# Spacing the row gathers of a mixture-of-experts layer along TensorE's work

## The chip, the cores and the metric

One core of a Trainium2 chip runs the whole program in one launch. The metric is the device time in microseconds (us); a kernel is judged by the median of its timed runs. All arithmetic is in 32-bit floating point.

## The reference

The input is 32 images of 128 channels of 56 x 56 pixels. Two layers follow each other.

```
# layer 0 (mixture of experts)
x  = depthwise 7x7 convolution, layer norm over channels      # 100352 tokens of 128 values
each token takes its best 2 of 8 experts; tokens are served in order of priority,
an expert takes at most cap = 15680 tokens
y  = gelu(x @ W1 + b1) @ W2 + b2                              # 128 -> 512 -> 128
out = input + x + layer_scale * (gate1 * y[slot1] + gate2 * y[slot2])

# layer 1, on that output
feat = gelu(batchnorm(3x3 dilated convolution, 128 -> 64 channels))
F2   = fft2(feat); attention of 8 heads from its Gram matrix; a gate from its real part
out  = concat(|ifft2(attention * F2)|, |ifft2(gate * F2)|) + input
```

## The kernel before

Layer 0 first convolves and routes all tokens and leaves the normalised tokens in HBM as `xf`. Then the eight experts run one after the other. An expert takes its tokens in 31 chunks of 512: `expert` multiplies a chunk by `W1` in four products (`ph`, L1034), applies the GELU on ScalarE (`hT`, L1037), multiplies by `W2` in sixteen products (`py`, L1049), adds the bias on VectorE (`yo`, L1065), scales by the gates on ScalarE and writes the rows to `yf` in HBM through SP's queue. `tick` is called after every second group of products and fills in other work. Experts 0 to 6 read their tokens with indirect gathers issued by POOL (`xg`, L1010); the last expert's tokens were packed ahead and come with ordinary transfers (`xlast`).

To combine, every token needs the rows of `yf` at its two slots. The tokens are cut into 112 rows of 7 x 128 tokens (`NRB`). A row needs 14 gathers (`NG`), each of 128 tokens (`y`, L437), 1568 in all, issued by POOL. `release` asks for the next gather. At a row's first gather it also loads the row's own tokens (`xa`, L430) through SP. `total` puts a row's two additions on VectorE (`xa`, L453) and then the write to `xsum` (L454) through SP. `bring` loads a finished row back (`xs`, L476), and asks for whatever that row still lacks.

Gathers are not let loose. `marks` remembers, for each gather asked, the TensorE instruction that was the last one noted in `step["pe"]` at that time. Gather n then waits for mark n minus `leash["n"]`:

```
        marks.append(step["pe"])
        gated(marks[max(0, n - leash["n"])], nc.gpsimd.indirect_dma_start(
```

The leash is 4 while the last expert runs and 16 in layer 1. The gathers begin in the last expert, where `ahead` may ask for two at each of the first three ticks of a chunk and one at every other chunk's fourth, as far as the rows of `yf` they may touch (`reach`) are written two chunks before. Six `y` buffers hold seven gathers each, so three rows are in flight.

Layer 1 handles images in 16 pairs. `front` of a pair places the rows: `place` transposes them (`pxs`, L1236), VectorE adds them to the padded input `xp` (L1240), and `taps` convolves (`pf`, L1251), with the GELU on ScalarE (`feat`, L1259). `back` does the transforms, each as `turn` (transposes `pt`, L1294, copied by VectorE to `mid`, L1281) and `product` (`pm`, L1302), with the Gram matrix (`pg`, L1326), and the attention (`pre`, `pim`, L1391 and L1392). The generator `front` of the next pair is run between the steps of `back` of this one. Each generator yields an amount of work w at the end of a step, and `worked(w)` counts it; for every `PACE` of it one gather is asked, so that one step may ask several at the same mark.

`PACE` divides the counted work of a pair by 98 (2 NP) and multiplies by 1.07, so that a pair asks for fewer gathers than it uses; the head start from the last expert makes up for it until it is used up, and then `bring` asks for what is missing.

POOL, VectorE, ScalarE and SP each take their instructions in the order of issue. SP's queue in layer 1 carries the xa loads, xsum writes, xs loads, the padded inputs and the output, one behind the other. A gather that waits on POOL holds the ones behind it; a sum that waits on VectorE holds the copies behind it.

Of the kernel before, what the change touches and what calls it, by code (L numbers as in the profile page):

```python
# [45 lines left out]
E = 8  # L46
# [28 lines left out]
def conv_seq_kernel(ctx: ExitStack, tc: tile.TileContext, t: dict, out: bass.AP, dbg: dict):  # L75
# [320 lines left out]

    NRB = NI // 2 * NB
    NG = 2 * NB
    begun_ = {}
    marks = []  # L400
    leash = {"n": 4}
# [5 lines left out]
    def reach(r):  # L407

        return (E - 1) * cap + min(cap, (r + 1) * FW)
# [48 lines left out]
        while made_["summed"] < NRB and made_["asked"] >= (made_["summed"] + 1) * NG + lag:  # L458
            total()

    def worked(w):

        work["since"] += w
        while work["since"] >= PACE:
            work["since"] -= PACE
            release()
            totals(NB)

    def bring(r):
        if r >= NRB or r < made_["rows"]:  # L470
# [10 lines left out]
            nc.sync.dma_start(out=xps[i], in_=t["xp"][pr + i * HI])  # L481
        return xps

    def ahead(i, of):

        if of == 1:
            totals(NG)
        for k in range(2 if of < 4 else i % 2):
            if i * 512 < reach(made_["asked"] // NG) - (E - 1) * cap + 2 * 512:
                return  # L490
            release()

    slot1 = route2.tile([128, J], I32, name="slot1")
# [15 lines left out]
    if True:  # L509
# [514 lines left out]
                [(ns % 128, slice(full, full + 1))] if ns % 128 else []  # L1024
            )

        def expert(e, c0, gates, ns, xT, tick, before):


            hT = c2.tile([C, FF // C, 512], F32, name="hT")  # L1030
            mine = []
            for f in range(FF // C):
                ph = bank("ph")
                step["pe"] = nc.tensor.matmul(  # L1034
                    ph[:, :ns], lhsT=W1[:, e, f * C : (f + 1) * C], rhs=xT[:, :ns], start=True, stop=True
                )
                gelu = nc.scalar.activation(  # L1037
                    hT[:, f, :ns], ph[:, :ns], AF.Gelu, bias=b1t[:, e, f : f + 1]
                )
                mine.append(step["pe"])  # L1040
                if f % 2:
                    tick()
            with tc.issue_after(gelu.ins):
                before()
            py = bank("py")
            for q in range(-(-ns // 128)):
                n = min(128, ns - q * 128)
                for f in range(FF // C):
                    step["pe"] = nc.tensor.matmul(  # L1049
                        py[:n, q * C : (q + 1) * C],  # L1050
                        lhsT=hT[:, f, q * 128 : q * 128 + n],
                        rhs=W2[:, e, f, :],
                        start=(f == 0),
                        stop=(f == FF // C - 1),
                    )
                mine.append(step["pe"])
                if q % 2:
                    tick()
            mine += mine[-1:] * (8 - len(mine))
            spots.append(mine)  # L1060
# [24 lines left out]
            return after  # L1085
# [35 lines left out]
        for e in range(E):  # L1121
# [31 lines left out]

            def tick():
                state[0] += 1
                if e == E - 1:
                    state[2] += 1
                    ahead(i, state[2])
                with tc.issue_after(begun.ins):
                    while state[1] < len(todo) and state[2] * slots_ < state[0] * whole:  # L1160
                        todo[state[1]]()
                        state[2] += share.get(todo[state[1]], 0.7)
                        state[1] += 1

            for i, c0 in enumerate(chunks):
                if i + 1 < len(chunks):
                    then = fetch(ids, chunks[i + 1], e == E - 1)
                elif e + 1 < E:
                    then = fetch(ids2, 0, e + 1 == E - 1)
                if e in (E - 3, E - 2):  # L1170
                    for n in range(2):
                        if 2 * (i + (e - E + 3) * len(chunks)) + n < NC:
                            put(0, 2 * (i + (e - E + 3) * len(chunks)) + n)
                state[2] = 0 if e == E - 1 else state[2]
                left = expert(e, c0, gates, *now, tick, left)
                now = then
            assert state[1] == len(todo)
            if e + 1 < E:
# [50 lines left out]
    def place(r, xps):  # L1229
        xs, rb = rows.pop(r), r % NB  # L1230
        for m0 in range(0, NB, 4):
            nm = min(4, NB - m0)
            pt = bank("pxs")
            pv = pt[:, : nm * 128].rearrange("p (q m s) -> p q m s", m=nm, s=P8)
            for m in range(nm):
                nc.tensor.transpose(pv[:, :, m, :], xs[:, m0 + m, :], ident)  # L1236
            for i in range(2):
                px = interior(xps[i], rb * P8, P8)[:, :, m0 * P8 : (m0 + nm) * P8]
                pi = pv[:, i * P8 : (i + 1) * P8].rearrange("p r m s -> p r (m s)")
                step["dve"] = nc.vector.scalar_tensor_tensor(  # L1240
                    out=px, in0=pi, scalar=bC, in1=px, op0=ALU.add, op1=ALU.add
                )

    def front(pr, xps, feat):


        def taps(pf, g, k0):
            for k in range(k0, k0 + 3):
                o = ((k // 3) * 3 + 8 * g) * RP + (k % 3) * 3
                for i in range(2):  # L1250
                    step["pe"] = nc.tensor.matmul(  # L1251
                        pf[i * DD : (i + 1) * DD, : 8 * W],
                        lhsT=cw[:, k, :],
                        rhs=xps[i][:, o : o + 8 * RP].rearrange("p (h w) -> p h w", w=RP)[:, :, :W],
                        start=(k == 0),
                        stop=(k == 8),
                    )
            if k0 == 6:
                nc.scalar.activation(  # L1259
                    feat[:, 8 * g * W : 8 * (g + 1) * W], pf[:, : 8 * W], AF.Gelu, scale=bsc, bias=bsh  # L1260
                )
# [24 lines left out]
    def transform(src, n, m, by, to, copy, more=None):  # L1286
# [3 lines left out]
        def turn(i0):  # L1290
            ni = min(4, n - i0)
            pt = bank("pt")
            for i in range(ni):
                step["pe"] = nc.tensor.transpose(pt[:m, i * 128 : (i + 1) * 128], src(i0 + i), ident)  # L1294
            mid = ring.tile([128, 4, 128], F32, name="mid")
            dve(mid[:m, :ni, :].rearrange("p i c -> p (i c)"), pt[:m, : ni * 128])
            return i0, ni, mid

        def product(i0, ni, mid):
            pm = bank("pm")  # L1300
            for i in range(ni):
                step["pe"] = nc.tensor.matmul(  # L1302
                    pm[:, i * M : (i + 1) * M], lhsT=mid[:m, i, :], rhs=by, start=True, stop=True
                )
            copy(to(i0, ni), pm[:, : ni * M])  # L1305
            if more:
                more(i0, ni, mid)
# [11 lines left out]
    def back(pr, xps, feat):  # L1319
# [3 lines left out]

        def gram(j0, nj, F0):
            for j in range(nj):
                nc.tensor.matmul(  # L1326
                    pg, lhsT=F0[: 2 * W, j, :], rhs=F0[: 2 * W, j, :],
                    start=(j0 + j == 0), stop=(j0 + j == NT - 1),
                )

        yield from transform(
            lambda j: feat[:, j * 2 * W : (j + 1) * 2 * W], NT, 2 * W, rw,
# [53 lines left out]
        def attend(g):  # L1386
# [1 line left out]
            pre = bank("pre")  # L1388
            pim = bank("pim")
            ftf = feat[:, 8 * g * W : 8 * (g + 1) * W]  # L1390
            nc.tensor.matmul(pre[:, : 8 * W], lhsT=attn, rhs=ftf, start=True, stop=True)  # L1391
            step["pe"] = nc.tensor.matmul(pim[:, : 8 * W], lhsT=meanw, rhs=ftf, start=True, stop=True)  # L1392
            sr = d2.tile([128, 8 * W], F32, name="sr")
            nc.scalar.activation(sr, pre[:, : 8 * W], AF.Square)
            nc.scalar.activation(pim[:, : 8 * W], pim[:, : 8 * W], AF.Square)
# [90 lines left out]
    MAIN = 2 * (NT * (64 + 4 * KF) + KF * (64 + 4 * KF)) + NT * 128 + NB * 16 * W + 2 * -(-KF // 4) * 2 * KF  # L1486
    FRONT = NB * (NB * 64 + 9 * 8 * W)
    LEAD = MAIN // 6
    leash["n"] = 16
    PACE = (MAIN + FRONT) / (2 * NP) * 1.07  # L1490

    def pair(pr):
        return inputs(pr) if pr else first_inputs, d2.tile([128, NPIX], F32, name="feat")

    this = pair(0)
    for w in front(0, *this):
        worked(w)
    for pr in range(NI // 2):
        then, steps = None, iter(())
        if pr + 1 < NI // 2:  # L1500
# [3 lines left out]
        for w in back(pr, *this):  # L1504
            made += max(w, 0)
            goal = max(0, made - LEAD) * FRONT // (MAIN - LEAD)
            if w < 0:
                goal = max(goal, fed - w * 3 * 8 * W)
            worked(max(w, 0))
            while fed < goal:  # L1510
                f = next(steps, None)
                if f is None:
                    break
                fed += f
                worked(f)
        for w in steps:
            worked(w)
        this = then


# [122 lines left out]
```

## Time and profile before

| what | value |
|---|---|
| timed runs, median of 3 | 4856.02 us (4854.89 to 4864.45) |
| profiled execution | 5281.71 us |
| its span, first to last instruction | 5279.9 us |
| mean granted TensorE clock | 0.948 |
| first gather of `yf`, last expert | 2733 us |
| first transpose of layer 1 | 2989 us |
| gathers of `yf`: number, mean recorded time | 1568, 992 ns |
| two additions of a row: each | 1086 ns |

A page of the profile gives busy time per engine, then the costliest groups of instructions: line, engine, operation, tile written from tiles read, count, then busy time and mean duration, then the idle time of the engine just ahead of them and what ended most of it. Windows give the same sums for stretches of the span. In the chain of waits each step is followed back to what released it. The profiled execution is longer than the timed ones, so sums from it are made against its own time.

### The profile page before, as it was taken

How to read it: one execution, taken by the hardware profiler on the slowest of the kernel's cores; microseconds unless marked ns; L12 is line 12 of the kernel's file. 1: busy time of each engine (PE TensorE's matmuls, PEld its weight loads, DVE VectorE, ACT ScalarE, POOL GpSimd, SP SyncE). 2: the span in 40 equal slices, each digit the busy share in tenths (PEclk: the TensorE clock that was granted, in tenths of full speed). 3: DMA queues.
4: the chain of work that ended last, by engine and by line, in shares of the span. 5: the costliest groups of instructions: out<-in, count | busy, mean ns of one | idle time of the engine just before them, and what ended most of it. 6: DMA issues, size and time to landing. Idle time of an engine off the chain costs nothing.

```text
span 5279.9 us, 87289 instructions
## 1 busy us (share of the span) xinstructions
PE 4709.7 (89%) x32984; PEld 3221.7 (61%) x32984; DVE 2802.5 (53%) x5764; ACT 2111.7 (40%) x4260; POOL 2668.8 (51%) x2640
## 2 busy tenths in 40 slices
PE   7888835999999999999999899999998888888889
PEld 7777723777767777666666555555555554555556
DVE  4787787748585866431112235555554444444456
ACT  3576741444444444434443323333332222333234
POOL 0000043545554555666636666666666666666650
PEclk9999966999999999999999999999999899999999
DMA  9998940222222222233355546555555555565642
GB/s 254 272 264 253 268 109 22 64 66 64 65 64 64 67 65 67 76 92 87 89 167 154 136 123 161 159 159 161 159 161 156 157 159 147 138 162 153 166 137 58
DMA packets 767255, 705.22 MB, mean 134 GB/s; under 512 B 72752, under 2 KB 679089, under 8 KB 762741
## 3 DMA queue, kind: packets, MB, share of 16 engines
q1 hardware_dynamic: 596580, 487.54, 31.2%
q0 software_dynamic: 81664, 167.15, 14.0%
q10 hardware_dynamic: 88592, 44.96, 3.0%
q8 instruction: 261, 4.28, 0.3%
q14 instruction: 158, 1.29, 0.1%
HBM read 472.99 MB, written 226.39 MB: 132 GB/s over the span
## 4 chain that ended last, share of the span: by engine, by line
PE 59%; issue 10%; another core or an unknown queue 4%; POOL 4%; DVE 4%; ACT 3%; DMA 1%; DVEq 0%; POOLq 0%; SPq 0%; ACTq 0%
PE pf L1251 14%; PE py L1049 12%; PE ph L1034 11%; PE pm L1302 8%; PE pt L1294 4%; POOL xg L1010 3%; PE pg L1326 2%; ACT hT L1037 2%; PE pxs L1236 2%; PE pre L1391 2%; PE pim L1392 1%; PE pxt L1016 1%; DMA xg<-xf,ids 1%; DVE mid L1281 1%
## 5 line engine op out<-in xcount | busy, mean ns | idle before, releaser
L437 POOL DMA_INDIRECT y<-yf,slot x1568 | 1555.0, 992 | 902.0 <-issue 366.2
L1010 POOL DMA_INDIRECT xg<-xf,ids x861 | 939.0, 1091 | 781.9 <-PE ph L1034 436.1
L1037 ACT ACTIVATE hT<-ph,b1t 128x512 f32<-128x512 f32 (+1 forms) x992 | 655.5, 682 | 1241.4 <-PE ph L1034 1119.0
L1049 PEld LDWEIGHTS py<-W,hT 128*128 128x128 f32 x7872 | 958.2, 194 | 245.6 <-ACT hT L1037 149.1
L1049 PE MATMUL py<-W,hT 128*128 128x128 f32 x7872 | 1035.9, 283 | 59.0 <-ACT hT L1037 35.4
L1251 PE MATMUL pf<-xp,cw 128*64 128x448 f32 x4032 | 917.9, 562 | 6.5 <-issue 5.2
L1034 PE MATMUL ph<-xT,W 128*128 128x512 f32 (+1 forms) x1984 | 899.4, 593 | 2.9 <-issue 2.8
L1065 DVE TENSOR_TENSOR yo<-py,b2t 128x512 f32<-128x512 f32 (+2 forms) x256 | 170.2, 667 | 896.0 <-issue 739.2
L1281 DVE COPY mid<-pt 112x512 f32<-112x512 f32 (+3 forms) x480 | 311.1, 661 | 594.3 <-remote 213.7
L1034 PEld LDWEIGHTS ph<-xT,W 128*128 128x128 f32 x1984 | 357.5, 192 | 335.8 <-issue 331.4
L1251 PEld LDWEIGHTS pf<-xp,cw 128*64 128x64 f32 x4032 | 283.8, 138 | 436.6 <-issue 400.6
L217 POOL TENSOR_SCALAR y<-y,sd,nb 128x128 f32<-128x128 f32 x49 | 24.8, 519 | 689.6 <-DVE nb L209 689.6
L222 ACT ACTIVATE y<-y,nb,sd 128x128 f32<-128x128 f32 x735 | 288.7, 480 | 76.3 <-DVE nb L209 76.3
L1075 ACT ACTIVATE yo<-yo,gates 128x128 f32<-128x128 f32 (+1 forms) x984 | 312.4, 394 | 5.6 <-issue 3.8
L1305 ACT COPY T<-pm 128x464 f32<-128x464 f32 (+2 forms) x240 | 123.1, 520 | 458.4 <-PE pm L1302 316.2
L171 PE MATMUL psa<-xt,stay 112*64 112x98 f32 (+1 forms) x4608 | 235.6, 261 | 43.6 <-DVE y L179 23.8
L171 PEld LDWEIGHTS psa<-xt,stay 112*64 112x64 f32 (+1 forms) x4608 | 219.4, 145 | 60.5 <-DVE y L179 28.0
L1240 DVE SCALAR_TENSOR_TENSOR xp<-pxs,beta,xp 128x256 f32<-128x256 f32 x448 | 173.1, 445 | 135.2 <-PE pxs L1236 59.8
L453 DVE TENSOR_TENSOR xa<-xa,y 128x896 f32<-128x896 f32 x224 | 243.2, 1086 | 2.8
L1259 ACT ACTIVATE feat<-pf,bn_shift,bn_scale 128x448 f32<-128x448 f32 x112 | 81.0, 724 | 404.7 <-remote 195.7
L179 DVE TENSOR_TENSOR y<-psa,dwbB 128x392 f32<-128x392 f32 x256 | 140.8, 558 | 188.1 <-PE psa L171 150.9
L1302 PE MATMUL pm<-ih,mid 116*128 116x112 f32 x928 | 151.2, 311 | 96.2 <-DVE mid L1281 71.3
(410 smaller groups left out, 6211.1 us busy)
## 6 DMA issues: line engine op xcount, KB each, us to landing
xt<-in_x_dram SPq DMA_DIRECT2D x256, 392.0 KB
yf<-yo SPq DMA_DIRECT2D x240, 256.0 KB
xp<-in_xp_dram SPq DMA_DIRECT2D x32, 1832.0 KB
xa<-xf SPq DMA_DIRECT2D x112, 448.0 KB
xsum<-xa SPq DMA_DIRECT2D x112, 448.0 KB
xs<-xsum SPq DMA_DIRECT2D x112, 448.0 KB
xf<-y ACTq DMA_DIRECT2D x42, 1024.0 KB
y<-yf,slot POOLq DMA_INDIRECT x1568
```

What stands on the lines that cost most here:

```text
L171: nc.tensor.matmul(ps[h * 64 : (h + 1) * 64, c * TG : (c + 1) * TG], lhsT=wts[b][:, c4 + c, :], rhs=xv[: PKS[b], c, h, :, b * NB : b * NB ...
L222: nc.scalar.activation(yi, yi, AF.Identity, scale=sd[:, i : i + 1], bias=nb[:, i : i + 1])
L437: gated(marks[max(0, n - leash["n"])], nc.gpsimd.indirect_dma_start(out=begun_[r][1][-1][:, m, :], out_offset=None, in_=yf[: 1 + reach(r), :],
L453: nc.vector.tensor_tensor(out=xs, in0=xs, in1=y, op=ALU.add)
L1010: paced(q, nc.gpsimd.indirect_dma_start(out=xg[:n, q, :], out_offset=None, in_=xf, in_offset=bass.IndirectOffsetOnAxis(ap=ids[:n, c0 + q : ...
L1034: step["pe"] = nc.tensor.matmul(ph[:, :ns], lhsT=W1[:, e, f * C : (f + 1) * C], rhs=xT[:, :ns], start=True, stop=True)
L1037: gelu = nc.scalar.activation(hT[:, f, :ns], ph[:, :ns], AF.Gelu, bias=b1t[:, e, f : f + 1])
L1049: step["pe"] = nc.tensor.matmul(py[:n, q * C : (q + 1) * C], lhsT=hT[:, f, q * 128 : q * 128 + n], rhs=W2[:, e, f, :], start=(f == 0), sto ...
L1075: nc.scalar.activation(yo[:n, q], yo[:n, q], AF.Copy, scale=gates[:n, c0 + q : c0 + q + 1])
L1251: step["pe"] = nc.tensor.matmul(pf[i * DD : (i + 1) * DD, : 8 * W], lhsT=cw[:, k, :], rhs=xps[i][:, o : o + 8 * RP].rearrange("p (h w) -> ...
L1281: step["dve"] = nc.vector.tensor_copy(to, of)
L1302: step["pe"] = nc.tensor.matmul(pm[:, i * M : (i + 1) * M], lhsT=mid[:m, i, :], rhs=by, start=True, stop=True)
```

## The change

A gather is now asked for at the TensorE instruction that completes a pace of work. `beat(w, ins)` replaces `worked`: it notes the instruction as the mark, counts a weight for it (10 for a transpose, 19 for a transform or Gram product, 32 for a convolution product, 64 for an attention product), and asks for a gather when a pace is full. The transposes of `place` and the Gram products, which set no mark before, do now. The pace is the sum of these weights over a pair, divided by 98, times 1.1. The sums are asked for by `totals(NB)` at the ends of steps as before, but no longer within the loop of gathers. The leash in layer 1 is 8. In the last expert `ahead` is called after each of the four `ph` products and each of the four groups of `py`, and asks for one gather each time that `reach` allows; the sums of that expert are asked for ahead of each chunk.

```diff
-    def worked(w):
-
+    def beat(w, ins):
+
+        step["pe"] = ins
         work["since"] += w
         while work["since"] >= PACE:
             work["since"] -= PACE
             release()
-            totals(NB)
...
-    def ahead(i, of):
-
-        if of == 1:
-            totals(NG)
-        for k in range(2 if of < 4 else i % 2):
-            if i * 512 < reach(made_["asked"] // NG) - (E - 1) * cap + 2 * 512:
-                return
+    def ahead(i):
+
+        if i * 512 >= reach(made_["asked"] // NG) - (E - 1) * cap + 2 * 512:
             release()
...
                 mine.append(step["pe"])
+                spot()
                 if f % 2:
                     tick()
...
                 mine.append(step["pe"])
+                spot()
                 if q % 2:
                     tick()
...
-                left = expert(e, c0, gates, *now, tick, left)
+                if e == E - 1:
+                    totals(NG)
+                left = expert(e, c0, gates, *now, tick, left, lambda: ahead(i) if e == E - 1 else None)
...
-                nc.tensor.transpose(pv[:, :, m, :], xs[:, m0 + m, :], ident)
+                beat(TURN, nc.tensor.transpose(pv[:, :, m, :], xs[:, m0 + m, :], ident))
...
-    leash["n"] = 16
-    PACE = (MAIN + FRONT) / (2 * NP) * 1.07
+    leash["n"] = 8
+    PACE = (4 * (NT + KF) * (TURN + PROD) // 2 + NT * PROD + 2 * NB * WIDE + NP * TURN + 18 * NB * TAP) / (2 * NP) * 1.1
...
     for w in front(0, *this):
-        worked(w)
+        totals(NB)
```

The other products (`pf`, `pt`, `pm`, `pg`, `pre`, `pim`) are wrapped in `beat` in the same way, and the other calls of `worked` become `totals(NB)`.

More of the change, by code (lines that the diff above doesn't have):

```diff
@@ L398, in conv_seq_kernel @@
     NG = 2 * NB
+    TURN, PROD, TAP, WIDE = 10, 19, 32, 64
     begun_ = {}
@@ L1025, in spans, with expert @@
             )
-        def expert(e, c0, gates, ns, xT, tick, before):
+        def expert(e, c0, gates, ns, xT, tick, before, spot):
             hT = c2.tile([C, FF // C, 512], F32, name="hT")
@@ L1155, in tick @@
                 state[0] += 1
-                if e == E - 1:
-                    state[2] += 1
-                    ahead(i, state[2])
                 with tc.issue_after(begun.ins):
@@ L1173, in conv_seq_kernel @@
                             put(0, 2 * (i + (e - E + 3) * len(chunks)) + n)
-                state[2] = 0 if e == E - 1 else state[2]
-                left = expert(e, c0, gates, *now, tick, left)
+                if e == E - 1:
+                    totals(NG)
+                left = expert(e, c0, gates, *now, tick, left, lambda: ahead(i) if e == E - 1 else None)
                 now = then
@@ L1250, in taps @@
                 for i in range(2):
-                    step["pe"] = nc.tensor.matmul(
+                    beat(TAP, nc.tensor.matmul(
                         pf[i * DD : (i + 1) * DD, : 8 * W],
@@ L1256, in taps @@
                         stop=(k == 8),
-                    )
+                    ))
             if k0 == 6:
@@ L1293, in turn @@
             for i in range(ni):
-                step["pe"] = nc.tensor.transpose(pt[:m, i * 128 : (i + 1) * 128], src(i0 + i), ident)
+                beat(TURN, nc.tensor.transpose(pt[:m, i * 128 : (i + 1) * 128], src(i0 + i), ident))
             mid = ring.tile([128, 4, 128], F32, name="mid")
@@ L1301, in product @@
             for i in range(ni):
-                step["pe"] = nc.tensor.matmul(
+                beat(PROD, nc.tensor.matmul(
                     pm[:, i * M : (i + 1) * M], lhsT=mid[:m, i, :], rhs=by, start=True, stop=True
-                )
+                ))
             copy(to(i0, ni), pm[:, : ni * M])
@@ L1325, in gram @@
             for j in range(nj):
-                nc.tensor.matmul(
+                beat(PROD, nc.tensor.matmul(
                     pg, lhsT=F0[: 2 * W, j, :], rhs=F0[: 2 * W, j, :],
                     start=(j0 + j == 0), stop=(j0 + j == NT - 1),
-                )
+                ))
         yield from transform(
@@ L1390, in attend @@
             ftf = feat[:, 8 * g * W : 8 * (g + 1) * W]
-            nc.tensor.matmul(pre[:, : 8 * W], lhsT=attn, rhs=ftf, start=True, stop=True)
-            step["pe"] = nc.tensor.matmul(pim[:, : 8 * W], lhsT=meanw, rhs=ftf, start=True, stop=True)
+            beat(WIDE, nc.tensor.matmul(pre[:, : 8 * W], lhsT=attn, rhs=ftf, start=True, stop=True))
+            beat(WIDE, nc.tensor.matmul(pim[:, : 8 * W], lhsT=meanw, rhs=ftf, start=True, stop=True))
             sr = d2.tile([128, 8 * W], F32, name="sr")
@@ L1508, in conv_seq_kernel @@
                 goal = max(goal, fed - w * 3 * 8 * W)
-            worked(max(w, 0))
+            totals(NB)
             while fed < goal:
@@ L1514, in conv_seq_kernel @@
                 fed += f
-                worked(f)
+                totals(NB)
         for w in steps:
-            worked(w)
+            totals(NB)
         this = then
```

## The prediction

> **What bounds the kernel now.** I read the page first, then the windows by stage, the waits of POOL, the chain of the last expert, and one timeline.
>
> ```profile
> PE 4709.7 (89%) x32984; PEld 3221.7 (61%) x32984; DVE 2802.5 (53%) x5764; ACT 2111.7 (40%) x4260; POOL 2668.8 (51%) x2640
> ...
> L437 POOL DMA_INDIRECT y<-yf,slot x1568 | 1555.0, 992 | 902.0 <-issue 366.2
> ...
> L453 DVE TENSOR_TENSOR xa<-xa,y 128x896 f32<-128x896 f32 x224 | 243.2, 1086 | 2.8
> ```
>
> TensorE is the busiest engine. The sums that use the gathers never waited for them: 2.8 us of idle in 224. So a gather is not late anywhere; what it can do is disturb TensorE, or sit badly. The windows are four stretches of layer 1:
>
> ```profile
> 3200.00:3600.00 400.00, 369.65 (x2185) 223.81 (x2183) 201.14 (x348) 128.51 (x215) 254.91 (x253) 0.95 0.59 158
> 3600.00:4000.00 400.00, 369.15 (x2187) 222.07 (x2184) 203.60 (x349) 130.47 (x217) 260.35 (x259) 0.97 0.59 160
> 4000.00:4400.00 400.00, 346.88 (x2012) 214.22 (x2010) 187.15 (x321) 112.97 (x190) 254.77 (x258) 0.93 0.57 154
> 4400.00:4800.00 400.00, 351.87 (x2012) 213.41 (x2012) 192.47 (x325) 114.83 (x193) 255.77 (x263) 0.94 0.59 158
> ```
>
> The first bracket is TensorE's instructions, the fifth POOL's. From 4000 us on TensorE gets through 8% less work (2012 against 2186) while POOL does as many gathers per us. That is the main lead. In the order of the built program, between the first attention products (L1391) of one pair and the next, POOL's gathers wait for marks of that pair 86 times in each of the first six pairs and 96 to 98 times in each of the next eight. By the starts of L1391 in the timeline, the first six take 133.3, 135.3, 135.7, 140.9, 133.2 and 132.6 us (mean 135.2), the next eight 146.8 to 154.6 (mean 149.8). The pace of 1.07 falls behind; from the seventh pair each row's remaining gathers are forced by `bring`, several on one mark.
>
> ```profile
> POOL y L437 <- issue: 324.0, 1033, 2.9
> POOL y L437 <- PE pm L1302: 146.6, 123, 3.6
> ```
>
> In layer 1, 1033 gathers followed the one before after 0.3 us of issue: POOL works in back-to-back runs of 1.25 us a gather. The longest stalls are of this kind, at 4109, 4264, 4416 and 5010 us, all in the later pairs:
>
> ```profile
> 4118.19 0.72 ACT L1259 ACTIVATE feat<-pf,bn_shift,bn_scale 128x448 f32<-128x448 f32 x1 [17.35 <-remote]
> ...
> 4120.38 0.98 PE L1302 MATMUL pm<-ih,mid 116*128 116x112 f32 x3 [10.96 <-DVE mid L1281]
> ```
>
> The convolution that this GELU waits for is recorded as ended at 4107.96; a gather that waits for the same product started at 4118.43, after a run of 17 back-to-back gathers. The last expert shows the same with nothing else changed:
>
> ```profile
> 2715.21 3.44 PE ph L1034 x8
> ...
> 2722.92 3.44 PE ph L1034 x8
> ...
> 2730.63 3.44 PE ph L1034 x8
> ...
> 2738.34 4.75 PE ph L1034 x8
> ...
> 2758.03 8.23 another core or an unknown queue x2
> ```
>
> A chunk takes 7.71 us until the first y gathers (2733 us); then 10 to 15 us alternates with 7.7.
>
> **What the Trainium skill says.** "Perfetto Trace Analysis", section "DMA Instruction — SWDGE (GPSIMD)": a gather's recorded time ends with its descriptors, not its data. The trace agrees: 0.99 us recorded, while the bytes of its queue, counted in order, land 5.4 us (median) and at most 10.8 us after its start. "TensorE: Matmul & The Clock Gate", table at its head: the queue is 64 deep, so a record may stand ahead of the work; the gather held until 4118 by a product recorded as over at 4107.96 agrees. Same page, "The cost: per-tile semaphore tail": about 26.3 ns per increment. The trace doesn't show that: after a convolution product that raises the semaphore the next starts 0.376 us later, after one that doesn't 0.376 (medians).
>
> **The change part by part.** The matmuls and their order stay but for 276 of 18813 places; what moves is which product each gather waits for, where sums stand, and thus the SP and DVE order.
>
> 1. Last expert. 6.5 gathers a chunk become 8. Gathers whose mark is ahead of layer 1's first transpose: 191 before, 218 after, +27. Price: from 2750 to 2950 us TensorE did 921 instructions; a chunk has 44 (8 of L1034, 32 of L1049, 4 of L1016) and takes 7.71 us undisturbed, so 921 are 161 us of work and 39 us were lost beside 135 gathers, 0.29 us each: 27 x 0.29 = +8 us. Upper end: the slope of step 3, 1.24 us, +33.
> 2. Pairs 1 to 6: 86 gathers become 89 to 90, about +3.2 each, 19 in all. At 0.29 us +6, at 1.24 us +24. I take +8.
> 3. Pairs 7 to 12: 96 to 98 become 89 to 90; the 13th 93; the 14th stays at 98. Slope between the two groups: (149.8 - 135.2) / (97.8 - 86) = 1.24 us a gather. Six pairs x 8.5 x 1.24 = -63, the 13th 5 x 1.24 = -6: -69. Lower end, if only the 0.29 counts: -16. The forcing by `bring` is over except in the last two pairs, and 1250 of 1293 marks carry one gather where 452 of 859 did (from gather 220), so I stay near the full: -60.
> 4. Semaphore. Products that raise it go from 5189 to 6204. By the trace nothing; by the skill's price an estimate of 1015 x 26.3 ns = 27 us if all were on the path. I take 0, keeping 0 to 27.
> 5. POOL's extra waits: 445 more semaphore instructions at 0.02 us are 9 us spread over 2400 us on an engine that stood waiting for others some 440 us in layer 1. 0.
> 6. Leash 16 to 8. A gather may start later, so the sum is nearer. Static distance from the awaited product to the sum, on before's times: least 17.6 us before, 9.9 after; median 31.8 before, 23.9 after. Measured slack from landing to the second addition was 10.4 us at least; less 7.7 it is 2.7. Cost 0. If that cover went, the DVE sum would wait, behind it `mid` and `xp`, then TensorE; and SP, which holds the xsum write and what is queued behind it. At most ten rows x 3 us = 30. Waiting gathers also hold later gathers on POOL; the same slack covers them.
> 7. SP: xsum writes and xa loads move by a few places; TensorE wants their rows two rows later, some 18 us. At layer 1's start the small loads (beta, cw) stay behind the same two xs loads, so that 8.8 us stall stays: 0.
>
> Sum: +8 + 8 - 60 = -44 us on the profiled 5281.71 (span 5279.9 plus 1.8 around it). The timed runs are shorter: median 4856.02, 0.92 of it. Scaled: -40, so **4816 us**. The profile may exaggerate the disturbance, since what it adds (425 us) is of the size of 1568 x 0.28 us.
>
> **Rivals.** (a) Forecast: late bunching goes, -40; for it the 8% drop at 4000 us and the stalls there alone. (b) The cost is a fixed price per gather wherever it stands: 1.24 in all steps gives +33 + 24 - 69 = -12, scaled -11, 4845; for it, that gathers per us are the same in all four windows; against it, 0.29 in the last expert. (c) Disturbance is mostly the profile's own: nothing but the ends stays, 4856 +- 9. (d) Slower: POOL becomes the bound of the last expert. Eight gathers need 8 x 1.25 = 10.0 us a chunk. That decides once a chunk takes under 10 us and the backlog exceeds the 14 to 22 places between ask and sum (about 20 us). With unprofiled chunks at 8.2 us (the mean of experts 1 to 4 in the profile, by the starts of L1034) the backlog is 26 x 1.8 = 47 us, 27 over the slack, and DVE holds TensorE by that: +27, plus 0 to 15 of steps 4 and 6, with layer 1 gaining little: about 4888. Against it: 9.5 us a chunk in the profile. That the change doesn't do what it says is excluded by the order of the marks.
>
> **How the numbers follow.** (a) 0.55, (b) 0.15, (c) 0.12, (d) 0.18. About 0.2% (10 us) is what a measurement of this kernel can tell from no change. Faster: all of (a) and half of (b) and a bit of (c), 0.66; same: the rest of (b) and (c), 0.16; slower: 0.18. (a) alone spans 4770 to 4843: the lower end if pairs 7 to 13 become like 1 to 6 in full (7 x 14.6 = -102, with +8 scaled -86), the upper if half of step 3 comes (-30 + 16, scaled -13). The range takes in (b) and (c) and half of (d): 4765 to 4872.
>
> **What would show it.** Right: TensorE's instructions per 400 us alike (about 2150) up to 4900 us; pairs 7 to 12 near 138 us; TensorE's waits of 10 us and more for `mid` gone; fewer than 1033 back-to-back gathers; last expert's chunk 9.6 to 10 us. Wrong: pairs still at 150 us with 89 gathers (the bunching wasn't it); L453 with tens of us of idle (leash too short or rival d); chunk beyond 10.5 us; layer 1 as before in the profile and yet slower runs.

## The result, and the profile after

| kernel | median of the timed runs | ratio to before, 95% interval |
|---|---|---|
| before | 4860.24 us (14 runs, 4854.89 to 4865.42) | |
| changed | 4867.59 us (14 runs, 4863.34 to 4874.26) | 1.0015 [1.0008, 1.0022] |

The forecast was 4816 us. The changed kernel is some 7 us slower, within what was called the same. Three more comparisons are told below: two repeat this, and in the last one, on another chip, the change was 40 us faster than the kernel before, the difference that was forecast. The result lies inside the range of the prediction, 4765 to 4872 us, but by luck: the range reached so far up only to take in half of rival (d).

The profiled execution of the changed kernel took 4864.57 us, so it stands for the timed ones. That of before, 5281.71 us, didn't: it is 8.7% above the median of the timed ones. The kernel before was therefore profiled again (first experiment): 4862.44 us. The comparison of stages uses this second profile.

The page of the changed kernel, the lines that answer to those shown of before:

```profile
PE 4528.4 (93%) x32984; PEld 3139.9 (65%) x32984; DVE 2801.9 (58%) x5764; ACT 2140.0 (44%) x4260; POOL 2682.7 (55%) x2640
...
L438 POOL DMA_INDIRECT y<-yf,slot x1568 | 1566.7, 999 | 566.3 <-issue 231.1
...
L454 DVE TENSOR_TENSOR xa<-xa,y 128x896 f32<-128x896 f32 x224 | 243.7, 1088 | 138.6 <-DMA y<-yf,slot 126.4
```

The sums, which had not waited in the first profile (2.8 us), now wait 138.6 us, nearly all for a gather's data. The windows of the changed kernel say where TensorE (first bracket) is short:

```profile
2750.00:2950.00 200.00, 150.75 (x795) 100.20 (x794) 49.13 (x82) 61.58 (x123) 153.37 (x154) 0.87 0.60 150
3200.00:3600.00 400.00, 400.00 (x2545) 250.57 (x2543) 234.32 (x403) 142.24 (x236) 300.91 (x303) 1.00 0.70 191
3600.00:4000.00 400.00, 399.99 (x2444) 238.35 (x2444) 230.18 (x393) 152.62 (x251) 295.99 (x296) 1.00 0.67 180
4000.00:4400.00 400.00, 399.99 (x2467) 242.19 (x2466) 234.43 (x403) 146.50 (x244) 297.14 (x296) 1.00 0.66 177
4400.00:4800.00 400.00, 397.30 (x2451) 243.70 (x2450) 224.96 (x385) 138.91 (x231) 254.50 (x252) 0.99 0.59 160
```

In layer 1 TensorE is full. Around the end of the last expert, 2750 to 2950 us, it is busy for three quarters of the time (150.75 of 200 us).

### The profile page after: what moved, and what is told of

The parts are those of the page before. It is cut to its first block, busy times and chain, and to the rows that moved or that the text cites. A ratio compares the mean times of both kernels' runs of the same rounds, so it can differ in the third digit from the quotient of the medians.

```text
span 4862.8 us, 87748 instructions
## 1 busy us (share of the span) xinstructions
PE 4528.4 (93%) x32984; PEld 3139.9 (65%) x32984; DVE 2801.9 (58%) x5764; ACT 2140.0 (44%) x4260; POOL 2682.7 (55%) x2640
## 5 line engine op out<-in xcount | busy, mean ns | idle before, releaser
L1034 ACT ACTIVATE hT<-ph,b1t 128x512 f32<-128x512 f32 (+1 forms) x992 | 676.1, 682 | 1100.3 <-PE ph L1031 1074.0
L1047 PEld LDWEIGHTS py<-W,hT 128*128 128x128 f32 x7872 | 940.6, 192 | 169.3 <-issue 121.3
L1047 PE MATMUL py<-W,hT 128*128 128x128 f32 x7872 | 987.1, 279 | 21.4 <-DVE yo L1064 21.1
L1248 PE MATMUL pf<-xp,cw 128*64 128x448 f32 x4032 | 880.8, 548 | 8.2 <-DVE xp L1237 7.8
L1064 DVE TENSOR_TENSOR yo<-py,b2t 128x512 f32<-128x512 f32 (+2 forms) x256 | 170.1, 667 | 714.2 <-issue 642.4
L454 DVE TENSOR_TENSOR xa<-xa,y 128x896 f32<-128x896 f32 x224 | 243.7, 1088 | 138.6 <-DMA y<-yf,slot 126.4
L1013 PE MATMUL pxt<-ident,xg 128*128 128x128 f32 (+1 forms) x984 | 195.2, 278 | 27.5 <-DMA xg<-xf,ids 27.5
```

Of the source, the lines that this page charges most:

```text
L454: nc.vector.tensor_tensor(out=xs, in0=xs, in1=y, op=ALU.add)
L1034: gelu = nc.scalar.activation(hT[:, f, :ns], ph[:, :ns], AF.Gelu, bias=b1t[:, e, f : f + 1])
L1047: step["pe"] = nc.tensor.matmul(py[:n, q * C : (q + 1) * C], lhsT=hT[:, f, q * 128 : q * 128 + n], rhs=W2[:, e, f, :], start=(f == 0), sto ...
L1248: beat(TAP, nc.tensor.matmul(pf[i * DD : (i + 1) * DD, : 8 * W], lhsT=cw[:, k, :], rhs=xps[i][:, o : o + 8 * RP].rearrange("p (h w) -> p h ...
```

## The experiments

The expectations speak of Theory P and Theory M. P is rival (d) of the prediction: eight asks in a chunk are more than POOL can issue, the sums on VectorE wait, and TensorE behind them. M: the semaphore raises of the moved marks cost time, at the price estimated in step 4 of the prediction. Every other letter is explained in the expectation that uses it; Theory S of the first experiment is not the rival S of the later ones. Ratios are to the kernel before on the same chip.

**The kernel before, once more.**

> The kernel before, unchanged, profiled once more. Theory S (the stalls of the first profile belonged to that execution, and layer 1 is full of TensorE work): a span near 4860 us, TensorE busy over 398 of 400 us between 3200 and 4400, pairs at 119 to 122 us whether 86 or 98 gathers fall in them. Theory F (the prediction: forced, bunched gathers slow TensorE): again above 5200 us, or, if shorter, pairs 7 to 14 at least 5 us longer than pairs 1 to 6.

Measured: 4862.44 us. Its windows and the line of its sums:

```profile
2750.00:2950.00 200.00, 189.47 (x1116) 123.69 (x1115) 61.57 (x109) 71.72 (x142) 152.73 (x156) 0.97 0.63 161
3200.00:3600.00 400.00, 399.99 (x2441) 238.85 (x2441) 228.21 (x392) 153.49 (x253) 290.11 (x293) 1.00 0.65 176
3600.00:4000.00 400.00, 399.60 (x2460) 241.19 (x2456) 238.11 (x408) 144.54 (x240) 299.80 (x299) 1.00 0.68 183
4000.00:4400.00 400.00, 385.47 (x2332) 231.60 (x2332) 223.80 (x379) 135.11 (x225) 306.02 (x307) 0.99 0.66 181
4400.00:4800.00 400.00, 384.39 (x2382) 237.13 (x2379) 213.93 (x366) 135.46 (x226) 256.96 (x255) 0.99 0.58 155
```

```profile
L453 DVE TENSOR_TENSOR xa<-xa,y 128x896 f32<-128x896 f32 x224 | 243.8, 1088 | 109.2 <-DMA y<-yf,slot 98.6
```

In the stretches from 3200 and from 4000 us the first profile had 2185 and 2012 instructions of TensorE, and this one has 2441 and 2332. TensorE is full up to 4000 us, and the sums wait already before the change. The chunks of the last expert take 7.7 us to the end (the first 8.4). By the starts of the attention products (L1391), the pairs take 119 to 122 us up to the ninth (the first 124.5), then 130.0, 127.3, 126.6, 129.9 and 126.9: the late pairs are longer by some 7 to 8 us here, not 15. So neither theory holds whole: the span is that of Theory S, but pairs 10 to 14 are longer than the early ones by more than the 5 us of Theory F.

**Each part alone.** Only the last expert's part:

```diff
-                    ahead(i, state[2])
...
+                if e == E - 1:
+                    totals(NG)
+                left = expert(e, c0, gates, *now, tick, left, lambda: ahead(i) if e == E - 1 else None)
```

> Only the last expert's part of the change: eight asks a chunk, one at each product group. Theory P (POOL cannot keep up with eight gathers in a 7.7 us chunk and the sums hold VectorE): slower than before by 5 to 20 us, sums (L449 to L454) idle for 80 us and more waiting for gathers, chunks of 10 us and more near the end of the expert. Theory M (the marks and semaphores of layer 1 cost): within 3 us of before.

Measured: 4889.27 us, ratio 1.0052 [1.0039, 1.0064]: 26 us slower, more than Theory P's 5 to 20. Its signs came: in the last expert the sums idle 88.5 us, and chunks take up to 17.9 us.

Only the part in layer 1 (the last expert asks as before):

```diff
+    def beat(w, ins):
...
-    leash["n"] = 16
+    leash["n"] = 8
```

> Only layer 1's part: beat, its weights, pace 1.1, leash 8; the last expert asks 6.5 a chunk as before. Theory P: between 10 us faster and 3 us slower than before, with no idle of the sums in the last expert beyond before's. Theory M (about 1000 more products raise the semaphore[...]): 7 to 27 us slower. Theory F: at least as slow as before, since the forcing by bring starts by the tenth pair.

Measured: 4857.02 us, 0.9988 [0.9980, 0.9996]; repeated later on another chip, 4854.32 us, 0.9984 [0.9977, 0.9991]. So the two parts have opposite signs, and Theory M's 7 to 27 us slower fall. Nor does the gain hide such a cost: 857 of the 1015 added raises are in this kernel, and its pairs 1 to 10 take 120.6 us in the mean, as pairs 2 to 9 of the kernel before do, where the price of step 4 would be some 1.5 us a pair. Among the versions that compute everything this is the only one clear of before in two comparisons, by about 6 us, and some 12 us faster than the changed kernel where both ran on one chip.

The place of the loss shows in the changed kernel's timeline, VectorE only (start, duration, instruction, idle before and what ended it):

```profile
2841.93 0.68 DVE L1014 COPY xT<-pxt 128x512 f32<-128x512 f32 x1
2846.16 1.09 DVE L454 TENSOR_TENSOR xa<-xa,y 128x896 f32<-128x896 f32 x1 [3.55 <-DMA y<-yf,slot]
2853.81 1.09 DVE L454 TENSOR_TENSOR xa<-xa,y 128x896 f32<-128x896 f32 x1 [6.55 <-DMA y<-yf,slot]
2854.82 0.68 DVE L1064 TENSOR_TENSOR yo<-py,b2t 128x512 f32<-128x512 f32 x1
2855.42 0.68 DVE L1014 COPY xT<-pxt 128x512 f32<-128x512 f32 x1
```

and one line of TensorE from the same stretch:

```profile
2855.65 1.62 PE L1047 MATMUL py<-W,hT 128*128 128x128 f32 x6 [2.95 <-DVE yo L1064]
```

A row's two sums sit in VectorE's order ahead of the chunk's bias addition `yo` (L1064) and of the copy `xT` for the next chunk. They wait 3.55 and 6.55 us for gathers, so `yo` ends at 2855.50, and the next `py` products start only then. POOL meanwhile starts a gather each 1.25 us without a gap (0.94 us and 0.30 us of issue):

```profile
2850.88 0.94 POOL L438 DMA_INDIRECT y<-yf,slot  x1 [0.30 <-issue]
2852.12 0.94 POOL L438 DMA_INDIRECT y<-yf,slot  x1 [0.30 <-PE ph L1031]
2853.37 0.94 POOL L438 DMA_INDIRECT y<-yf,slot  x1 [0.30 <-issue]
```

Chunks are 7.7 us until the 19th, then between 7.7 and 21.2.

| stage, us | before, second profile | changed | last expert only | layer 1 only |
|---|---|---|---|---|
| last expert, first L1034 to first transpose of layer 1 | 237.6 | 273.5 | 269.1 | 237.6 |
| from there to the first L1391 | 106.7 | 117.7 | 117.4 | 110.3 |
| the next 15 starts of L1391 (first to last) | 1843 | 1804 | 1822 | 1835 |

(Lines by their numbers in the kernel before.) The change is +36 + 11 - 39 = +8 by stage, against the measured +7. (What stands ahead of the last expert is the same program; it still differs by up to 6 us between these executions.) The +36 follow from a count: ahead of the last `yo` of the expert stand the sums of 11 rows before and of 13 rows in the change, 28 gathers more, and 28 x 1.30 us, POOL's time for a gather in a long run, are 36 us. The 11 rows just fit: 154 x 1.30 us after the first gather, at 2658.4, are 2858.6, and the last of their sums starts at 2858.1 without a wait. The part in layer 1 alone can't have the 39 us: its head start is 160 gathers, not 186, so the asks run short from the eleventh pair on (127.2, 134.3, 125.0, 126.5 us) as they did before.

**Six asks in a chunk instead of eight.**

```diff
-                spot()
+                if f < 3:
+                    spot()
...
-                spot()
+                if q < 3:
+                    spot()
```

> The changed kernel, but the last expert asks at six of its eight product groups: 6 x 1.25 = 7.5 us of POOL in a 7.7 us chunk, so the head start falls from 219 to 170 gathers. Theory P: no sum waits in the last expert, its chunks stay at 7.7 us to the end, 5 to 20 us faster than the changed kernel as long as layer 1 swallows the 49 gathers (98 a pair are 122 us of POOL against 120 of TensorE, so up to 10 us may come back at the end). Theory M: no gain on the changed kernel, 7 us above before or more.

Measured: 4869.12 us, 1.0015 [1.0009, 1.0022]. Windows of 2700 to 2850 us, of this kernel and then of the last expert's part alone:

```profile
2700.00:2850.00 150.00, 149.99 (x867) 108.75 (x865) 41.21 (x54) 75.79 (x157) 114.35 (x118) 1.00 0.70 175
```

```profile
2700.00:2850.00 150.00, 135.49 (x755) 98.05 (x753) 41.68 (x54) 66.87 (x136) 114.34 (x118) 0.97 0.70 174
```

POOL has the same 118 instructions in both; TensorE has 867 against 755. So P's mechanism is right: with six asks the last expert is whole again (all chunks 7.7 us, no sum waits there). But P's total is missed, since nothing was won: the gathers not asked ahead came back as six pairs of 127.6 to 128.6 us. The total is near the one that Theory M gave, but the part in layer 1 alone, with all the marks of this kernel in layer 1, has shown that it isn't the raises.

**Sums later in the last expert** (20 places behind instead of 14).

```diff
-                    totals(NG)
+                    totals(NG + 6)
```

> The changed kernel with the last expert's sums asked for 20 gathers after their row instead of 14. Theory P (it is the sums, waiting on VectorE for late gathers, that pass POOL's backlog on to TensorE): the sums idle less than 60 us in the last expert where they idled some 90, TensorE's long chunks shrink, the expert ends 12 to 25 us earlier and the run is 10 to 25 us faster than the changed kernel. Rival (POOL's own time sets the end whatever waits): the sums wait as long further on and the end stays within 4 us of the changed kernel.

Measured: 4867.06 us, 1.0014 [1.0008, 1.0021]. The first sum that waits is at 2787.5 us instead of 2743.5; in the last expert the sums idle 64.7 us instead of 89.3, but the expert still takes 270.2 us (the changed kernel 269.8 to 273.5 in three executions). So the rival is right and P's gain of 10 to 25 us is missed: POOL's own time sets the end. With either lag the sums of 13 rows, 182 gathers, stand ahead of the expert's last `yo`. In the changed kernel the first gather starts at 2652.6; 182 x 1.30 us later is 2889, and the last of these sums starts at 2890.4. The backlog is only met later.

**The leash, and a shorter pace.**

```diff
-    leash["n"] = 8
+    leash["n"] = 16
```

> The changed kernel with the leash in layer 1 at 16 as before. Theory P: the last expert is untouched (leash 4 there), layer 1 is full of TensorE work, so within 4 us of the changed kernel, or up to 8 us faster where the first pair's sums still wait. Theory L (the short leash is worth something): 5 us slower or more than the changed kernel.

Measured: 4861.60 us, 1.0004 [0.9996, 1.0012], against 1.0015 [1.0008, 1.0022] of the changed kernel. At most some 5 us hang on the leash, and rather in favour of the longer one, so Theory L falls; the two intervals overlap.

```diff
-    PACE = (...) / (2 * NP) * 1.1
+    PACE = (...) / (2 * NP) * 1.05
```

on the part in layer 1 alone, with leash 8 and with 16:

> Layer 1's part alone, as in e_layer1_only, with the pace at 1.05 where that had 1.1: 93 or 94 gathers in every pair, none forced by bring. Theory Q (a pair takes the longer of TensorE's 119 to 121 us and POOL's gathers times 1.3 us): every pair at 119.5 to 122 us, the sums' idle time below 30 us, 20 to 35 us faster than before (six late pairs lose their 6 to 8 us). Theory R (late pairs are slow because of something else than their count): the last five pairs stay at 125 us and more, within 10 us of e_layer1_only.

> The kernel of e_pace105 with the leash at 16 instead of 8. Theory Q: POOL's waits for TensorE's marks in layer 1 fall from about 200 us and every gather starts up to eight places earlier, but TensorE is full, so within 4 us of e_pace105. Theory L (the short leash is what keeps transfers from colliding): 5 us slower or more.

Measured: 4859.88 us, 0.9999 [0.9991, 1.0008], and 4859.07 us, 0.9996 [0.9989, 1.0004]: the leash makes no difference here, so Theory L falls once more. Here a pair asks for 93 or 94, nothing is forced before the last pairs, and the first fourteen pairs of the first of the two take 121.1 to 127.1 us, mean 123.2 (94 x 1.30 = 122). Theory Q's 20 to 35 us faster are missed, and so are its 30 us of idle sums (196 measured): with TensorE and POOL both nearly full, a pair takes some 1 us more than the longer of the two. Theory R's late pairs of 125 us and more didn't come either. Spread evenly, the gathers cost what they cost bunched at the end: no difference to the unspread part beyond 5 us. This speaks for the number of gathers in a pair as what costs, and against their spacing.

**More and fewer gathers.** That led to Theory G: POOL's own time per gather, 1.30 us in a long run, is the floor. Two edits of the part in layer 1 alone test it. One more gather in each of rows 16 to 111, in `release`:

```diff
+        if k == NB and r >= 16:
+            nc.gpsimd.indirect_dma_start(
+                out=begun_[r][1][-1][:, NB - 1, :],
...
```

and one less:

```diff
+        if k == NG - 1 and r >= 16:
+            return
```

> The layer-1 part alone, with one gather more in each of the rows 16 to 111 (96 more; it fetches the same tokens as the row's eighth gather, into a place that the fourteenth overwrites, so nothing else changes). Theory G (POOL's time per gather, about 1.30 us at a stretch, is the floor of layer 1, and TensorE is full only while a pair needs fewer than some 92 gathers): 96 x 1.30 = 125 us, less the 35 us that POOL still has spare in layer 1 of the layer-1 part alone (1.325 against 1.30 us an interval, 1400 gathers): +90 to +125 us on its 4857, so 4945 to 4985; sums wait in nearly every pair. Rival S (each gather disturbs TensorE by a fixed 0.3 to 0.67 us): +28 to +64, 4885 to 4920. Rival H (gathers lie hidden beside TensorE): under +15.

> The layer-1 part alone, with the fourteenth gather of each of the rows 16 to 111 left out (96 fewer, and the second addition of these rows takes six of its seven places, so part of the combination is not computed). Theory G: the pairs of 125 to 134 us at the end become 119 to 122 like the others, about -28 us, and no more, because TensorE is then full: 4825 to 4835; sums wait nowhere in layer 1. Rival S (0.67 us per gather everywhere): -64, about 4793, and the pairs of 121 us shrink as well. Rival H: within 8 us of 4857.

Measured: 5409.84 us, 1.0159 [1.0138, 1.0181], and 5183.49 us, 0.9737 [0.9712, 0.9761]. These two ran on a chip on which the kernel before itself takes 5330.93 us in seven timed runs, so the numbers in us that were expected don't apply; they are read below. They were repeated together with the changed kernel and the part alone:

> The changed kernel as it is, beside the three others. Where before takes about 4860 us: 4867 again. Where before takes about 5330 us, as on the chip of the previous two experiments: Theory D (on that chip each gather takes TensorE some 1.2 us of work, and more where several follow one another; so it is the chip, not the profiler, that the first profile shows) has the prediction's own sum hold there: -44 us on before, 5270 to 5310. Rival E (spreading is worth nothing there either; only the number of gathers counts): within 10 us of before.

> The layer-1 part alone. Where before takes about 4860 us: 4857 again. Where before takes about 5330 us: Theory D: about -50 (the sum without the last expert's +8): 5260 to 5300. Rival E: within 10 us of before.

> The layer-1 part alone with 96 gathers more, again. Where before takes about 4860 us: Theory G (POOL's 1.30 us a gather is the floor): +90 to +125 us on the layer-1 part alone, 4945 to 4985, with waiting sums in nearly every pair; rival S (a fixed 0.3 to 0.67 us each): +28 to +64; rival H (hidden): under +15. Where before takes about 5330 us: 5410 again, +110 on the layer-1 part alone by Theory D (96 x 1.2).

> The layer-1 part alone with 96 gathers fewer (part of the combination is not computed), again. Where before takes about 4860 us: Theory G: about -28 us on the layer-1 part alone, 4825 to 4835, and no more, because TensorE is then full; rival S: -64, about 4793; rival H: within 8 us of 4857. Where before takes about 5330 us: 5183 again, -110 on the layer-1 part alone by Theory D.

On this chip before takes 4860.39 us. Measured: 4866.51 (1.0012 [1.0003, 1.0020]), 4854.32, 4953.25 (1.0184 [1.0167, 1.0201]) and 4812.98 us (0.9899 [0.9882, 0.9915]). Against the part alone, 96 gathers more are +98.9 us, in G's band of 90 to 125 and well outside S and H. 96 fewer are -41.3 us, between G's -28 and S's -64. Two windows with 96 more, then two with 96 fewer:

```profile
3600.00:4000.00 400.00, 393.75 (x2357) 233.49 (x2355) 220.66 (x377) 146.91 (x243) 306.40 (x307) 0.99 0.66 176
4000.00:4400.00 400.00, 374.25 (x2213) 225.37 (x2214) 209.93 (x359) 126.02 (x210) 306.13 (x309) 0.96 0.64 173
```

```profile
3600.00:4000.00 400.00, 400.00 (x2485) 243.79 (x2482) 237.76 (x410) 145.84 (x243) 274.35 (x275) 1.00 0.66 177
4000.00:4400.00 400.00, 400.00 (x2513) 247.74 (x2512) 229.78 (x398) 141.83 (x235) 299.76 (x301) 1.00 0.71 194
```

With more, POOL stands at 306 us of 400 and 307 to 309 instructions in both, which is one per 1.30 us with the issue between them, and TensorE gives way: 2357 and 2213 of some 2450. With fewer, TensorE is full and the pairs are 119.1 to 121.7 us to the last. G's -28 was too small because it left out what the pairs of 121.4 us (now 120.4) and the fifteenth (114.4, now 107.1) still had to give; with the 31 us of the four late pairs that makes the 41. So a pair takes about the longer of TensorE's 119 to 122 us and 1.30 us times its gathers, and some us more where the two are close; they cross near 92.

**The changed kernel on such another chip.** What was open was whether the prediction's sum holds where before takes 5330 us.

> The changed kernel once more, for the chip it meets. Where before takes about 5330 us: Theory D (there each gather costs TensorE some 1.2 us, more where several follow one another) 5270 to 5310; Rival E (spreading is worth nothing there either) within 10 us of before. Where before takes about 4860 us: 4867 again, which tells nothing new.

Measured: 4869.36 us against 4859.38, 1.0018 [1.0010, 1.0026]; a chip like the first, nothing new.

> The changed kernel once more, for the chip it meets. Where before takes about 5330 us: Theory D (there each gather costs TensorE some 1.2 us, more where several follow one another) 5270 to 5310; Rival E (spreading is worth nothing there either) within 10 us of before. Where before takes about 4860 us: 4867 again, nothing new.

Measured: 5292.13 us (5285.36 to 5293.04, four runs) against 5332.41 us of before (5315.87 to 5343.09, six runs), ratio 0.9927 [0.9902, 0.9952]. Theory D's band was met and E falls: there the change is 40 us faster (26 to 52 by the interval), as forecast. Its windows:

```profile
2750.00:2950.00 200.00, 158.65 (x754) 111.94 (x753) 41.73 (x54) 64.69 (x137) 133.42 (x137) 0.88 0.53 136
3200.00:3600.00 400.00, 364.37 (x2164) 220.91 (x2168) 202.03 (x348) 122.91 (x207) 257.48 (x258) 0.97 0.58 158
3600.00:4000.00 400.00, 367.17 (x2164) 221.75 (x2158) 203.61 (x344) 123.22 (x207) 255.14 (x260) 0.96 0.59 162
4000.00:4400.00 400.00, 363.81 (x2113) 215.21 (x2110) 201.46 (x340) 127.15 (x213) 254.74 (x255) 0.96 0.58 158
4400.00:4800.00 400.00, 369.09 (x2130) 216.86 (x2129) 205.45 (x353) 128.62 (x214) 257.72 (x257) 0.96 0.56 152
```

2113 to 2164 instructions in each stretch: the drop at 4000 us is gone, and the pairs are 134.5 to 145.7 us, mean 139.8. Here POOL has room (255 of 400, no sum waits beyond 3.1 us in all); what is short is TensorE.

## Why the prediction was wrong

Its mechanism in layer 1, gathers that slow TensorE, most where a pair has many of them, exists on the chips where it was read. Two steps failed: the scaling of the sum, and within the sum step 1, to which some 40 of the 47 us between forecast and result belong.

The failure came first in **the step from the profile to the time**: "Scaled: -40". The profiled execution was 8.7% longer than the timed ones, and this was taken as a factor on all steps. It was another regime: TensorE slowed by the gathers and POOL with slack, where the timed runs had TensorE full and POOL close to its floor. A factor of 0.92 doesn't lead from one to the other. Rival (c), "disturbance is mostly the profile's own: nothing but the ends stays", was close for the timed chips, though it isn't the profiler: on two chips all timed runs are as long as that (5331 and 5332 us), and profiled executions on the others are as short as the timed ones.

**Step 1** (+8) is the term that was wrong on both kinds of chip. Measured: +36 in the last expert and +11 at the head of layer 1. Where the prediction put a price of disturbance, 0.29 us for each gather more, the timed runs show POOL's own time, 1.30 us for each gather that a sum in the expert waits for. That is rival (d), with its place and its mechanism, given 0.18. Its total of 4888 us was for the whole change and is 20 us too long; that the part alone came to 4889.27 us is partly chance, since its pairs won 22 us that (d) didn't count. It was argued away with "9.5 us a chunk in the profile"; in the timed regime a chunk takes 7.7 us (the rival took 8.2), so eight asks at 1.25 us each overrun it by 2.3 us. On the chip of the last run the last expert took 343.2 us, where three executions with the asks of before took 290 to 294 (the first profile and the two with more and fewer gathers): +50, so the price of 0.29 us a gather was too low there too, by another way: no sum waits there, and why TensorE loses the 50 us is part of what stays open. The sign of being wrong that the prediction named, "chunk beyond 10.5 us", came true there (343.2 us over 30.6 chunks of 512 are 11.2).

**Steps 2 and 3.** The static counts (86 and 98 before, 89 to 90 after) were right. The slope of 1.24 us a gather was right for its regime: between 96 gathers more and 96 fewer on such a chip lie 226.4 us, 1.18 us each (+79 and -147 us against before; the part alone, of which both are versions, was not run on that chip), and pairs 7 to 12 came to 139.1 us (predicted near 138). In the timed regime the step from 86 to 98 is worth 128.1 - 120 = 8 us, 0.67 a gather, because up to 92 the gathers lie under TensorE's time. Measured gain in the pairs: 39 us, where steps 2 and 3 together said 52 before scaling and 48 after.

**Steps 4 and 5** (raises, POOL's extra waits: 0) held: the part in layer 1 alone is faster than before, and in the changed kernel too a convolution product that raises the semaphore is followed after 0.376 us (median of 485). **Step 6** (leash: 0, at most 30) held within 5 us, though its landing time was read too long: counted back from the last packet of POOL's queue, a gather's data land 2.9 us (median) and at most 8.3 us after its start in the first profile, not 5.4 and 10.8. The 26 sums of the changed kernel that waited for a gather agree: they start 2.8 to 8.4 us after it, median 3.2. **Step 7** (SP's order: 0) was not tested by itself; the stages add up without it.

**Where the gain went.** On the timed chips the gathers run from 2658 to 4733 us before the change, 2075 us, and 1568 x 1.30 is 2038. POOL is 98% used from first to last, and from the start of the last gather the rest takes 126 to 128 us in the schedules compared here, 137 with the shorter pace. In the change it is 2083, with six asks 2078, with the part alone 2069, with the shorter pace 2056. A gather that is moved out of a late pair has to be paid in the last expert or in another pair; with the first gather where it is, no placement can win more than some 40 us, by this estimate, and this one won 39 in the pairs and lost 47 ahead of them.

**What stays open.** Why two chips take 5331 and 5332 us for the kernel that takes 4859 to 4863 us on four others (the clock granted is 0.94 to 0.95 and 0.97). They are not slower at everything. Up to 2140 us the four profiled executions of 5180 us and more run like the fourteen short ones, at the same mean clock (0.937 to 0.940 against 0.934 to 0.942), and experts 1 to 4 take 247 to 255 us each in both kinds. Expert 5 (counted from 0) takes 284 to 288 us against 244 to 248; there the packing of the last expert's tokens joins, and POOL's gathers go from 4 to 6 a chunk. Whether the number of gathers or the writes of the packing make the difference, and why on these chips alone, is not shown. In their traces an engine often starts long after the instruction that it waits for is recorded as over, its releaser being given as "remote"; these waits sum to 724 us in the first profile and 517 in the last run, the first of them stands at 2155 to 2209 us, in expert 5, and there is none in the second profile of before. Two lines of the last run, ScalarE's waits:

```profile
ACT hT L1034 <- remote: 119.5, 14, 12.1
ACT T L1302 <- remote: 86.0, 21, 6.7
```

Also open is how the -40 us there divide into stages. From the first profile to the last run the last expert loses 53 us and the pairs 1 to 14 win 52, no net gain; but the kernel before was timed on that last chip at 5332 us, 50 above the first profile, and wasn't profiled there. By stage this looks more like rival (b), one price for a gather wherever it stands: pairs 1 to 6 lose 22 us (forecast 8, upper end 24) and pairs 7 to 14 win 75 (forecast 60). That the -40 equals the forecast is therefore in part luck: if the last expert loses 50 us there, as estimated in step 1, the rest must have won some 90.

## What to carry to other kernels

Before a price is taken from a profile, set its time against the timed median: here, at 8.7% apart, it showed another regime, and its slopes couldn't be scaled. Ask which resource is full in each. For a stream that an engine issues itself, multiply its count by the time of one in a long run and compare with the stretch it has; at 98%, as here, moving its members can win no more than the 2% that are left. And where a stage's asks times their price exceed the stage's own time, a longer lag hid nothing here: six places more put the first wait off by 44 us, and the expert ended no earlier. Count how many of the stream's members the stage's last instruction stands behind.

## What the runs showed that was not expected

- One and the same program took 4859 to 4863 us on four chips and 5331 to 5332 us on two, and the sign of a change's worth differed between them: 1.0015 and 0.9927.
- A gather of 128 rows of 512 bytes keeps POOL 0.94 to 0.96 us in nearly nine cases of ten, plus 0.30 us of issue; the others take up to 2.6 us in the executions near 4860 us, so a long run goes at 1.30. The Trainium skill's "Perfetto Trace Analysis", section "DMA Instruction — SWDGE (GPSIMD)", says that the recorded time is the making of descriptors. That agrees: the record is POOL's load, and the sums' waits come later, from the data.
- On the chips of 5331 us each gather costs about 1.2 us of the run (226.4 us for 192) although POOL is recorded busy for only 255 us of 400, where it reaches 306 when it works without a gap.
- Between executions 420 us apart the order of the instructions of VectorE, ScalarE and POOL and of SP's transfers is the same to the last one (second profile of before against the first).
